# Attention scores begun before the last value block, four tiles of a quad handed to other engines, and a second norm issued later

## The chip, the cores and the metric

The kernel runs on one core of one Trainium2 chip. The metric is the device time of one execution in microseconds; the time of a kernel is the median over its runs. Engines are called PE (matmul; PEld is its weight load), DVE (VectorE), ACT (ScalarE), POOL (GpSimd) and SP (the queue that issues the DMAs).

## The reference

Two graph-attention layers are followed by one masked transformer layer over N = 4096 rows of D = 256, with 8 heads of 32. The change touches the transformer layer only.

```python
def _L1_gnn_ref(x, adj, w_qkv, w_proj, b_proj, w1, b1, w2, b2, g1, be1, g2, be2):
    n = x.shape[0]
    qkv = layer_norm(x, g1, be1) @ w_qkv
    qkv = qkv.reshape(n, 3, HEADS, HEAD_DIM)
    q, k, v = (qkv[:, 0], qkv[:, 1], qkv[:, 2])
    scores = jnp.einsum('nhd,mhd->hnm', q, k) * SCALE
    mask = (adj != 0)[None, :, :]
    scores = jnp.where(mask, scores, -jnp.inf)
    attn = jax.nn.softmax(scores, axis=-1)
    out = jnp.einsum('hnm,mhd->nhd', attn, v).reshape(n, DIM)
    x = x + out @ w_proj + b_proj
    h2 = layer_norm(x, g2, be2)
    ff = jax.nn.gelu(h2 @ w1 + b1) @ w2 + b2
    return x + ff
```

## The kernel before

The graph-attention layers take the first 1600 us and are left alone. `unshifted_transformer` then has three stages.

**q, k and v.** The rows are in eight blocks of 512 (`nb`). For each block the normed rows are turned (`ahead.turned`, PE transposes and an ACT copy into `hn`), and the PE forms k and then q (`i` = 1, 0; L1810), which ACT and DVE split into an fp16 head and remainder (`u_halves`, L1817 and L1818). SP writes these to `half_d` in DRAM and loads them back stacked for the scores (`u_k`, `u_q`, L1734); for the last three blocks all four copies come by DMA, for the others two come by DMA and DVE makes the other two (L1846). The values follow (L1829), and ACT copies them to `v_sb`. All eight PSUM banks serve this stage as one pool, `ps_q`. On SP the order is as written; the other engines' order is the scheduler's.

**Attention.** The order on every engine is written out by hand here. A quad is one query block of 512 rows with one head group of four heads (16 quads); a unit is one key tile of 128 in a quad (32 units a quad, 512 in all); each unit has two halves `u` of two heads. For each half the PE forms the scores (`u_ps`, eight matmuls, L1872; three buffers of two banks), ACT takes the exponential in place (L1882), and DVE multiplies by the mask into `u_e` (L1883; pool `work`, ten buffers). Two halves are treated otherwise in each quad: for tiles 0 and 16, first half, ACT writes the exponential to SBUF (L1885) and POOL multiplies it (L1886) by a mask that ACT made two units earlier (`keep_mask`, L1896).

The sums are split into parts of a quarter of the columns, which wait in the list `waiting` and are popped behind the scores, three in each half and sometimes four. `weigh` multiplies `u_e` by the values into `u_av`; `total` multiplies by ones into `u_dn`. For most pairs of tiles POOL first adds the two (`u_both`, L2095), and one total serves both; a pair for which `alone` holds gets two totals on the PE, straight from `u_e`:

```python
        def alone(mt):
            return mt // 2 % 8 == 7
```

At the end of a quad ACT copies `u_av` and `u_dn` out (L1920, L1937), and later DVE inverts the sums (L1946). `u_av` and `u_dn` have one bank each. In the last quad `load_early` brings the weights and rows for the next stage, and `rows_ready(k)` (two POOL products, L2016 and L2017) prepares the first two row blocks; the dictionary `ending` places this and the following steps.

**Output and feed-forward.** `project(k)` for the first two row blocks stands among the last sums of attention: 16 PE records (L2048), four DVE adds (L2056), then the second norm (DVE statistics L1514 and L1521, ACT square root L1526, DVE L1535 and L1543), and a POOL addition (L2065). `turn_first(c)` turns the two column halves of the first block through `u_av` (PE and ACT, L1556 and L1559). The feed-forward loop over eight blocks follows (L2186, L2193, L2206).

## Time and profile before

| | |
|---|---|
| time, median of 3 runs | 3123.89 us (3123.82 to 3124.47) |
| the profiled execution | 3124.94 us, span 3123.2 us |
| PE busy in the span | 3061.6 us (98%) |
| DVE busy | 2747.7 us (88%) |
| ACT busy | 2699.7 us (86%) |
| POOL busy | 1265.1 us (41%) |
| q/k/v stage | about 1602 to 1690 us |
| attention | 1693 to about 2863 us |
| feed-forward | from 2866 us |

Busy time is summed over stages with different limits, so it is read by stretch. In the groups of the profile a line gives the source line, engine, operation, what is written from what, count, busy time, mean length of one, and the idle time before it with what ended that. The timeline merges neighbours of one kind. The chain goes back from the last instruction to what released each step. A matmul with fp32 operands appears as two records.

### The profile page before, as it was taken

Reading aid. Unit: us, or ns where it says so; the run is one execution under the profiler, and the core shown is the slowest. Engines: PE = TensorE matmul, PEld = TensorE weight load, DVE = VectorE, ACT = ScalarE, POOL = GpSimd, SP = SyncE. Lnnn points to the kernel's source line nnn. Section 1 sums busy time; section 2 is a strip of 40 time slices with the busy share of each in tenths; the row PEclk is TensorE's granted clock in tenths of the full one; section 3 lists DMA queues with packets and bytes.
Section 4 is the critical chain, followed back from the end, with each engine's and each line's share of the span. In section 5 each row is a group of like instructions: output and inputs, shape, how many; then the busy total and the mean of one; then the engine's idle time right before and its main releaser. Section 6 shows DMA issues by size and latency. Waiting matters only on the chain.

```text
span 3123.2 us, 139201 instructions
## 1 busy us (share of the span) xinstructions
PE 3061.6 (98%) x63976; PEld 2713.3 (87%) x63976; DVE 2747.7 (88%) x3110; ACT 2699.7 (86%) x3370; POOL 1265.1 (41%) x568
## 2 busy tenths in 40 slices
PE   6999999999999999999999999999999999999998
PEld 5899999999889999999975888888888888887766
DVE  7999999999989999999985999999999999997220
ACT  6899999999899999999975999999999999996232
POOL 3300000000330000000002999999999999997110
PEclk8999999999999999999999999999999999999999
DMA  8666555431311213121145101010101110013210
GB/s 257 218 198 205 171 174 167 144 100 33 91 59 29 90 56 97 32 64 53 46 116 152 34 21 35 21 41 28 35 21 35 30 30 28 28 40 102 68 34 22
DMA packets 213171, 250.35 MB, mean 80 GB/s; under 512 B 89120, under 2 KB 133664, under 8 KB 212576
## 3 DMA queue, kind: packets, MB, share of 16 engines
q1 hardware_dynamic: 212576, 241.37, 25.1%
q8 instruction: 502, 8.22, 1.1%
q14 instruction: 93, 0.76, 0.1%
HBM read 198.84 MB, written 42.47 MB: 77 GB/s over the span
## 4 chain that ended last, share of the span: by engine, by line
PE 51%; ACT 1%; DVE 1%; issue 0%; DMA 0%; DVEq 0%; ACTq 0%
PE u_ps L1872 15%; PE u_av L1904 14%; PE u_dn L1904 8%; PE misc L2186 4%; PE misc L2206 4%; PE bank L1463 3%; PE misc L1810 2%; PE misc L1829 1%; ACT t L1122 1%; PE misc L2147 1%; PE misc L1556 0%; DVE t L1137 0%; DVE t L1124 0%; DVE u_e L1883 0%; PE u_ps L2048 0%
## 5 line engine op out<-in xcount | busy, mean ns | idle before, releaser
L1463 PE MATMUL bank<-vst,t 128*128 128x132 f16 x16384 | 1455.9, 220 | 3.6 <-DVE t L1137 2.7
L2095 POOL TENSOR_TENSOR u_both<-u_e 128x1024 f32<-128x1024 f32 x448 | 1047.9, 2388 | 805.1 <-DMA u_k<-half_d 775.6
L1463 PE MATMUL bank<-vst,mask 128*128 128x132 f16 (+1 forms) x10516 | 1372.3, 206 | 0.0
L1122 ACT ACTIVATE t<-s_b,g_terms 128x1024 int8<-128x1024 f32 x1234 | 1318.7, 1148 | 21.0 <-PE bank L1463 15.2
L1463 PEld LDWEIGHTS <-t 128*128 128x128 fp8e4 x16384 | 1186.3, 96 | 15.8 <-DVE t L1137 5.4
L1883 DVE SCALAR_TENSOR_TENSOR u_e<-u_mask,u_ps 128x1024 f32<-128x1024 uint8 x994 | 1131.5, 1213 | 26.8 <-ACT u_ps L1882 25.8
L1882 ACT ACTIVATE u_ps<-u_ps 128x1024 f32<-128x1024 f32 x994 | 996.4, 1008 | 93.0 <-PE u_ps L1872 33.6
L1463 PEld LDWEIGHTS <-mask 128*128 128x128 fp8e4 x10516 | 920.4, 98 | 0.0
L1137 DVE SCALAR_TENSOR_TENSOR t<-mask,t 128x2048 int32<-128x2048 int32 x256 | 587.9, 2296 | 74.8 <-ACT t L1122 66.4
L1872 PE MATMUL u_ps<-u_q,u_k 128*32 128x512 f16 x8192 | 632.4, 381 | 7.0 <-DVE u_e L1883 4.5
L1904 PE MATMUL u_av<-u_e,u_v 128*32 128x128 f32 x16384 | 602.9, 273 | 0.0
L1124 DVE TENSOR_SCALAR t<-s_b,g_terms 128x1024 fp8e4<-128x1024 f32 x814 | 590.1, 758 | 2.7 <-DMA s_b<-s_d 2.7
L1904 PEld LDWEIGHTS u_av<-u_e,u_v 128*32 128x32 f32 x16384 | 483.2, 110 | 120.6 <-issue 0.7
L1054 POOL TENSOR_TENSOR vst<-g_adj,vst 128x528 f16<-128x528 f32 x16 | 19.9, 1241 | 725.7 <-ACT g_big L1018 681.6
L1904 PE MATMUL u_dn<-u_both,u_ones 128*32 128x128 f32 x7168 | 279.2, 273 | 0.0
L1904 PEld LDWEIGHTS u_dn<-u_both,u_ones 128*32 128x32 f32 x7168 | 212.9, 110 | 52.1 <-issue 0.7
L1872 PEld LDWEIGHTS <-u_k 128*32 128x32 f16 x8192 | 229.5, 96 | 29.2 <-issue 8.9
L2193 ACT ACTIVATE u_hid<-misc,n_b 128x512 f32<-128x512 f32 x64 | 43.9, 687 | 140.3 <-PE misc L2186 140.3
L2206 PE MATMUL misc<-u_k,u_hid 128*128 128x256 f32 x512 | 111.8, 379 | 0.0
L2206 PEld LDWEIGHTS misc<-u_k,u_hid 128*128 128x128 f32 x512 | 96.7, 190 | 13.3 <-issue 0.5
L2186 PE MATMUL misc<-ln_cols,u_k 128*128 128x512 f32 x224 | 97.3, 592 | 0.0
L867 DVE TENSOR_SCALAR adj<-g_adj 128x1024 fp8e4<-128x1024 int32 x123 | 88.9, 723 | 3.8 <-DMA g_adj<-in_adj_dram 3.8
(186 smaller groups left out, 1919.2 us busy)
## 6 DMA issues: line engine op xcount, KB each, us to landing
g_adj<-in_adj_dram SPq DMA_DIRECT2D x123, 512.0 KB
s_b<-s_d SPq DMA_DIRECT2D x64, 512.0 KB
mask<-mask SPq DMA_DIRECT2D x128, 256.0 KB
u_mask<-mask SPq DMA_DIRECT2D x64, 256.0 KB
mask<-stage SPq DMA_DIRECT2D x48, 256.0 KB
half_d<-u_halves SPq DMA_DIRECT2D x32, 256.0 KB
u_q<-half_d SPq DMA_DIRECT2D x32, 256.0 KB
rows<-e_x SPq DMA_DIRECT2D x31, 256.0 KB
```

Of the source, the lines that this page charges most:

```text
L867: nc.vector.tensor_scalar(v.rearrange("p m r -> p r m"), loaded.pop((nb, c, i)), 1.0, -(2.0**-30), op0=ALU.min, op1=ALU.max, saturate=False,)
L1122: nc.scalar.activation(to.bitcast(I8), s, AF.Sign, bias=negd, scale=-1.0)
L1124: nc.vector.tensor_scalar(to, s, negd, -1.0, op0=ALU.is_ge, op1=ALU.mult, saturate=False)
L1137: nc.vector.scalar_tensor_tensor(both, m32.unsqueeze(1).to_broadcast(list(both.shape)), SIGNS, both, op0=ALU.bitwise_or, op1=ALU.bitwise_and,)
L1463: nc.tensor.matmul(to, left, right, start=k not in opened, stop=last)
L1872: nc.tensor.matmul(ps[r * O : (r + 1) * O, j, :], k_st[c][:, 2 * u + j, at : at + O], q_st[:, h, :], start=True, stop=True,)
L1882: nc.scalar.activation(ps, ps, AF.Exp, scale=SCALE)
L1883: nc.vector.scalar_tensor_tensor(e, mask, 0.0, ps, op0=ALU.not_equal, op1=ALU.mult)
L1904: nc.tensor.matmul(to[j * O : (j + 1) * O, at], lefts[j], es[j // 2][:, j % 2, at], start=first and part == 0, stop=last and part == PARTS ...
L2095: nc.gpsimd.tensor_tensor(both, es_of[i - 1][u], es_of[i][u], op=ALU.add)
L2186: nc.tensor.matmul(ph, w1_sb[:, k, f * P : (f + 1) * P], hn[:, k, :], start=(k == 0), stop=(k == DC - 1),)
L2206: nc.tensor.matmul(po[:, :D], hid[:, f, at : at + P], w2_sb[:, f, :], start=(f == 0), stop=(f == FC - 1),)
```

## The change

- **Scores earlier.** The values of the last row block are no longer formed in the q/k/v stage, but in the first units of attention (`last_values`: tiles 0 to 2 behind the scores of unit 1, tile 3 behind those of unit 2), through the banks of `u_av` and `u_dn`. Their inputs are kept in a `u_q` buffer (`hn_last`, and `wv_last`, loaded by two more DMAs). PSUM in the q/k/v stage becomes pools of six and two banks; the last block's k takes the six, its q the two. `work` moves to the right side of SBUF, where the buffers of the layers before were; `u_both` gets a pool of its own. `u_halves` has four buffers in place of three, and block 4's k joins those that come by DMA alone.
- **Other places in a quad.** The PE sums tiles 6, 7, 22 and 23 by itself in place of 14, 15, 30 and 31, and in the last quad tiles 30 and 31 too. POOL masks the second half of tiles 8 and 24 in place of the first half of tiles 0 and 16; the mask for it is made one unit ahead. `rows_ready(0)` moves from tile 15 of the last quad to tile 23.
- **Second norm later.** `project` is cut in two; the norm of the first block follows its projection as before, that of the second comes behind `turn_first(1)`.

```diff
-        if c == 0:
+        if to is not None:
+            self.hn[nb] = to
+        elif c == 0:
...
-            hv = qkv.enter_context(tc.tile_pool(name="u_hv", bufs=3))
-            ps_q = qkv.enter_context(tc.tile_pool(name="u_ps_q", bufs=8, space=PSUM))
+            hv = qkv.enter_context(tc.tile_pool(name="u_hv", bufs=4))
+            psums = [
+                qkv.enter_context(tc.tile_pool(name=f"u_ps_q{k}", bufs=n, space=PSUM))
+                for k, n in enumerate((6, 2))
+            ]
+            used = []
+            def bank(which=None):
+                used.append(None)
+                k = len(used) % 4 == 0 if which is None else which
+                return psums[k].tile([P, NB], F32, name="misc")
...
+            spare = blocks.tile([P, 4 * NB], F32, name="u_q")
+            hn_last = spare[:, : DC * NB].rearrange("p (c n) -> p c n", c=DC)
+            wv_last = spare[:, DC * NB : DC * NB + DC * D].rearrange("p (c e) -> p c e", c=DC)
...
+                if nb == 3:
+                    for c in range(DC):
+                        nc.sync.dma_start(
+                            wv_last[:, c], ahead.w_qkv[c * P : (c + 1) * P, 2 * D : 3 * D]
+                        )
...
-                        pq = ps_q.tile([P, NB], F32, name="misc")
+                        pq = bank(1 - i if nb + 1 == NNB else None)
...
-                for t in range(TB):
-                    pv = ps_q.tile([P, NB], F32, name="misc")
+                for t in range(TB) if nb + 1 < NNB else ():
+                    pv = bank()
...
-                            late = b >= NNB - 3
+                            late = b >= NNB - 4
...
-        work = scope.enter_context(tc.tile_pool(name="u_work", bufs=10))
+        work = scope.enter_context(tc.tile_pool(name="u_work", bufs=10, side="right"))
+        adds = scope.enter_context(tc.tile_pool(name="u_adds", bufs=6))
...
-            one = kept.pop((nb, c, mt), None) if u == 0 else None
+            one = kept.pop((nb, c, mt), None) if u == 1 else None
...
-        def alone(mt):
-            return mt // 2 % 8 == 7
+        def last_values(t):
+            at, name = (NNB - 1) * TB + t // 2 * 2, ("u_av", "u_dn")[t // 2]
+            if t % 2 == 0:
+                sums_of[name] = ps_a.tile([P, NB], F32, name=name)
+            to = sums_of[name]
+            for k in range(DC):
+                nc.tensor.matmul(
+                    to[:, t % 2 * D : (t % 2 + 1) * D],
+                    hn_last[:, k, t * P : (t + 1) * P],
+                    wv_last[:, k, :],
+                    start=(t % 2 == 0 and k == 0),
+                    stop=(t % 2 == 1 and k == DC - 1),
+                )
+            if t % 2 == 1:
+                nc.scalar.copy(
+                    v_sb[:, at : at + 2, :].rearrange("p t d -> p (t d)"), sums_of.pop(name)
+                )
+        def alone(i):
+            return units[i][2] // 2 % 8 == 3 or i + 2 >= len(units)
...
-            (units.index((NNB - 1, DC - 1, NT // 2 - 1)), 1): [lambda: rows_ready(0)],
+            (units.index((NNB - 1, DC - 1, 23)), 1): [lambda: rows_ready(0)],
...
                 lambda: project(0),
+                lambda: norm_rows(0),
             ],
             (last + 3, 0): [lambda: project(1)],
             (last + 3, 1): [lambda: turn_first(0)],
-            (last + 4, 1): [lambda: turn_first(1)],
+            (last + 4, 1): [lambda: turn_first(1), lambda: norm_rows(1)],
...
+        def norm_rows(k):
+            res = early[k][0]
             both = norms.moments(res)
...
-                    if u == 0 and i + 2 < len(units) and units[i + 2][2] % 16 == 0 and (
-                        units[i + 2] != (NNB - 1, DC - 1, NT // 2)
+                    for t in {2: (0, 1, 2), 4: (3,)}.get(2 * i + u, ()):
+                        last_values(t)
+                    if u == 0 and i + 1 < len(units) and units[i + 1][2] % 16 == 8 and (
+                        units[i + 1] != (NNB - 1, DC - 1, 24)
                     ):
-                        keep_mask(*units[i + 2])
-                    if i % 2 == 1 and not alone(mt):
+                        keep_mask(*units[i + 1])
+                    if i % 2 == 1 and not alone(i):
```

More of the change, by code (lines that the diff above doesn't have):

```diff
@@ L1596, in normed, with turned @@
         self.norms.normed(self.xs[nb], self.xs[nb], self.held.pop(nb))
-    def turned(self, nb, c, pt):
-        if c == 0:
+    def turned(self, nb, c, pt, to=None):
+        if to is not None:
+            self.hn[nb] = to
+        elif c == 0:
             self.hn[nb] = self.stage_p.tile([P, self.D // P, 512], F32, name="g_ft", tag="stage")
@@ L1798, in unshifted_transformer @@
                     for c in range(DC):
-                        ahead.turned(nb + 1, c, ps_q.tile([P, NB], F32, name="misc"))
+                        to = hn_last if nb + 2 == NNB else None
+                        ahead.turned(nb + 1, c, bank(), to)
+                if nb == 3:
[3 more added lines that the diff above has]
+                        )
                 if 2 < nb + 2 < NNB:
@@ L2088, in unshifted_transformer @@
                     es_of.setdefault(i, []).append(weights(*units[i], u))
-                    if u == 0 and i + 2 < len(units) and units[i + 2][2] % 16 == 0 and (
-                        units[i + 2] != (NNB - 1, DC - 1, NT // 2)
-                    ):
-                        keep_mask(*units[i + 2])
-                    if i % 2 == 1 and not alone(mt):
-                        both = work.tile([P, 2, NB], F32, name="u_both", bufs=6)
+                    for t in {2: (0, 1, 2), 4: (3,)}.get(2 * i + u, ()):
+                        last_values(t)
+                    if u == 0 and i + 1 < len(units) and units[i + 1][2] % 16 == 8 and (
+                        units[i + 1] != (NNB - 1, DC - 1, 24)
+                    ):
+                        keep_mask(*units[i + 1])
+                    if i % 2 == 1 and not alone(i):
+                        both = adds.tile([P, 2, NB], F32, name="u_both")
                         nc.gpsimd.tensor_tensor(both, es_of[i - 1][u], es_of[i][u], op=ALU.add)
@@ L2100, in unshifted_transformer @@
                     ready(total, i - 4, both_of.pop(i - 4))
-                if u == 1 and 0 <= i - 2 < len(units) and alone(units[i - 2][2]):
+                if u == 1 and 0 <= i - 2 < len(units) and alone(i - 2):
                     ready(total, i - 2, es_of[i - 2])
```

## The prediction

> **What bounds the kernel now.** I read the page's groups, the busy times by stretch, the timeline of VectorE (DVE), and the chain of work that ended last, in this order. A unit is one key tile of one quad (query block and head group); it has two halves, `u` = 0 and 1, of two heads each. The groups of the attention loop:

> ```profile
> L1883 DVE SCALAR_TENSOR_TENSOR u_e<-u_mask,u_ps 128x1024 f32<-128x1024 uint8 x994 | 1131.5, 1213 | 26.8 <-ACT u_ps L1882 25.8
> L1882 ACT ACTIVATE u_ps<-u_ps 128x1024 f32<-128x1024 f32 x994 | 996.4, 1008 | 93.0 <-PE u_ps L1872 33.6
> L2095 POOL TENSOR_TENSOR u_both<-u_e 128x1024 f32<-128x1024 f32 x448 | 1047.9, 2388 | 805.1 <-DMA u_k<-half_d 775.6
> ```

> The loop runs from 1693 to about 2850 us, so DVE's masking is busy 1131.5 of some 1157 us. The stretches show where the engines are not full:

> ```profile
> core 0: us, PE busy (x) PEld busy (x) DVE busy (x) ACT busy (x) POOL busy (x), PEclk, DMA share, GB/s
> 1602.00:1690.00 88.00, 88.00 (x310) 53.84 (x309) 53.23 (x126) 43.45 (x85) 0.00 (x0) 1.00 0.67 198
> 1690.00:1703.00 13.00, 6.75 (x111) 4.01 (x113) 7.05 (x7) 7.26 (x11) 2.77 (x2) 0.87 0.69 186
> 1711.80:1783.90 72.10, 72.10 (x2104) 59.08 (x2100) 70.58 (x63) 66.32 (x74) 70.24 (x31) 1.00 0.10 29
> ```

> The q/k/v stage (1602 to 1690) is full on the PE. The hand-over (1690 to 1703) is half empty on every engine. One quad, the last row, shows the PE at 72.10 of 72.10 and DVE at 70.58. DVE's timeline tells which of the two paces it (second column: length of the run, last: what ended the idle time):

> ```profile
> 1703.10 30.63 DVE L1883 SCALAR_TENSOR_TENSOR u_e<-u_mask,u_ps 128x1024 f32<-128x1024 uint8 x27 [0.72 <-ACT u_ps L1882]
> 1734.44 35.22 DVE L1883 SCALAR_TENSOR_TENSOR u_e<-u_mask,u_ps 128x1024 f32<-128x1024 uint8 x31 [0.71 <-ACT u_ps L1882]
> 1770.34 15.13 DVE L1883 SCALAR_TENSOR_TENSOR u_e<-u_mask,u_ps 128x1024 f32<-128x1024 uint8 x13 [0.69 <-ACT u_ps L1882]
> 1785.39 0.25 DVE L1946 RECIPROCAL u_inv<-u_dens 128x16 f32<-128x16 f32 x1
> ...
> 1806.65 35.19 DVE L1883 SCALAR_TENSOR_TENSOR u_e<-u_mask,u_ps 128x1024 f32<-128x1024 uint8 x31 [0.71 <-ACT u_ps L1882]
> 1842.56 15.02 DVE L1883 SCALAR_TENSOR_TENSOR u_e<-u_mask,u_ps 128x1024 f32<-128x1024 uint8 x13 [0.71 <-ACT u_ps L1882]
> ```

> Between the halves that GpSimd masks, DVE runs without a gap, one mask each (35.22 - 1.21) / 30 = 1.133 us. The PE needs less for a half: 0.43 us of scores and three parts of sums of 0.22, 1.09 us, with one extra part in each eight halves. So DVE paces these runs; a half given to GpSimd (a relief) saves 1.13 and loses 0.70 of idle, 0.43 net. Sixteen tiles take 1770.34 - 1734.44 = 35.90 us where no quad ends in between, and 1806.65 - 1770.34 = 36.31 where one does. The chain passes the same PE group at 1711.77 and, 15 quads later, at 2794.03: 72.15 us a quad. The hand-over in that chain (start, length, what):

> ```profile
> 1692.10 0.69 DVE u_halves L1818
> 1692.79 0.02 issue
> 1692.81 3.69 DMA half_d<-u_halves
> ...
> 1696.62 2.36 DVE u_e L1883 x2
> ...
> 1703.10 3.49 DVE u_e L1883 x3
> ```

> The first `u_e` waits for the last write of `half_d` to land: its memory was `u_halves`.

> [...] DVE paces quads in which the PE shows 72.10 of 72.10. [...] in the trace ScalarE (ACT) writes a relief half's exponentials to `u_e` first (L1885, 1.03 us), and then GpSimd multiplies (2.41 us). [...] L1883 has one input in each memory and takes 1,157 to 1,224 ns while POOL is 97% busy, so I move POOL's work without changing DVE's price. [...] after the 3.43 us wait at 1697.89, eight score matmuls took 1.05 us at 1699.02 in place of 0.62.

> **The change, part by part.**

> *1. Early first scores.* The PE reaches the last block's value matmuls (L1829) at 1686.94. Afterwards the first scores stand there. Their six PSUM banks were last used by block 7's k halves, two q-groups (3.4 us) earlier; and `u_e`, now on the right side, no longer lies on `u_halves`. Walking the queues from there, with durations of before:
> - ACT casts the last q piece (0.58) to 1687.75; DVE subtracts (0.69) to 1688.45. Score 1 is done at 1686.94 + 0.62; its exp (1.01) ends 1688.76; masks 1 to 3 start at 1688.8, 1689.9, 1691.1.
> - The PE does three score halves, then values of tiles 0 to 2 (0.87 each) from 1688.45, when q frees the bank: to 1691.1. Score 4 starts there; ACT first copies the values out (0.57), and exp 4 ends 1692.75: mask 4 starts at 1692.8 after 0.6 of idle, mask 5 at 1693.95.
> - Score 6 stands behind score 5 (0.43), the fourth values (0.87) and three parts (0.65): 1693.5. Behind ACT's second copy, exp 6 ends 1695.16; mask 6 starts at 1695.2.

> Before, mask 6 started at 1703.10 (the run after the 0.72 gap). From there both are paced by DVE: **7.9 us** gained. Bounds 7.4 and 8.4: one copy of 0.5 more in the way, or one less.

> What this needs lies beside other work. Two 128 KB loads of value weights and four more k loads (block 4) go to SP's queue in a stage with a DMA share of 0.67; they delay block 3's and block 6's `half_d` writes by 0.4 to 0.5 us of issue each, and block 4's k is read only after 16 tiles (36 us). Without that cover the PE would stop on a k load, 1 to 3 us. Four DVE copies of 0.7 fall away where DVE is 60% busy: nothing. The fourth `hv` buffer takes away a 1.5 us wait of ACT that the PE did not feel: nothing. The 6+2 split of banks keeps the reuse distance at eight tiles: nothing. POOL's first sum waits for the same `half_d` writes; they now leave after 1688.45 and land about 3.7 us later, at 1692.4, when the third mask ends.

> *2. Other places in the quad.* The same counts a quad: 62 masks on DVE, two on POOL, 28 sums on POOL, four tiles that the PE sums alone. Before, the relief (tile 0) falls on the end of a quad, right after ACT's two copies of `u_av` and `u_dn` come due (0.48 us of ACT each). ACT is then already what DVE waits for: the 13 masks at 1770.34 take 15.13 where 12 x 1.133 + 1.21 = 14.81, and 15.02 at 1842.56: 0.2 to 0.3 lost a quad. Moved to tile 8, the quad's end lies amid a DVE-paced run, where a score can start as soon as the mask three halves ahead is done: exp is ready 1.21 + 0.06 + 0.66 + 1.01 = 2.94 us after that mask starts, and is wanted after 3.40. A copy of 0.48, less the 0.21 that ACT is idle in each half, fits into 0.46. The reciprocal (0.17) stays. So a quad becomes 2 x 35.90 + 0.17 = 71.97, or about 71.85 if the second half also shortens the relief's idle: 0.18 to 0.30, I take 0.25, x 15 = 3.75. Tile 8 of the first quad is relieved too (31 reliefs, not 30): 0.43. Sum **4.2**, bounds 1 and 6.

> The wait that is added: `weigh` of tile 8 needs GpSimd's half one half later in the unit. Before, the product ended at 1735.93 and tile 16's values began at about 1739.25: 3.3 us of slack, so about 2.2 remain; POOL has just had the alone pair's 4.5 us free. Cost nothing. The Sign (0.53 of ACT) is moved, not added, but for one.

> *3. Last pair alone.* Two more totals less one: 32 PE records, 0.87 us, against a GpSimd sum that was late anyway; the PE has some slack in the last quad: **0.2 to 0.87** lost, I take 0.5. `rows_ready(0)` (two POOL products, 2.4 each) goes to tile 23, again into an alone pair's hole.

> *4. Later second norm.* At the end the ACT queue holds the second block's Sqrt ahead of the first block's turned copy:

> ```profile
> 2863.85 0.36 DVE L1521 BATCH_NORM_AGGREGATE n_mean<-n_stats 128x2 f32<-128x6 f32 x4
> 2864.24 0.30 ACT L1526 ACTIVATE n_mean<-n_mean,n_eps 128x4 f32<-128x4 f32 x1 [6.35 <-DVE n_mean L1521]
> 2864.45 0.76 ACT L1559 ACTIVATE u_q<-u_av,n_be,n_g 128x512 f32<-128x512 f32 x1
> ...
> 2866.95 0.28 PEld L2186 LDWEIGHTS misc<-u_q,u_k 128*128 128x128 f32 x1 [0.74 <-ACT u_q L1559]
> ```

> The transposes for the first copy ended at 2862.49, so without the Sqrt it runs 2862.5 to 2863.3. The PE's sums end at 2863.28, second transposes to 2863.7; ACT copies `u_den` (0.57) and turns the second half by about 2864.85. The second weight load of the feed-forward stage moves from 2866.95 to 2864.85: **2.1** gained (1.2 if the copy of `u_den` falls badly, 2.3 at most). Late next is the second block's norm, by some 0.8 us; its transposes come at 2884, so nothing. The first GELU waits behind it, with eight PSUM banks for the PE.

> Sum: 7.9 + 4.2 - 0.5 + 2.1 = 13.7. The profiled execution took 3124.94 us (span 3123.2), 1.05 above the median of the runs, 3123.89; I take the 13.7 from either: 3111.2 as profiled, **3110.2** as median.

> **Rivals.**
> - *Placement gives nothing:* DVE paces as before and the copies' cost turns up elsewhere. For it: the relief's 0.70 of idle stays in any place. Against: the boundary's extra 0.41 us is plainly in the trace. 3110.2 + 4.2 = 3114.4.
> - *The change doesn't do what it says at the start:* `u_e`, or a neighbour in its queue, still waits for the last `half_d` write (1692.4). Mask 1 then starts 3.6 later: 3113.8. For it: such a wait was there before. Against: the memory is another.
> - *Slower: a new PE wait at the end of each quad.* `u_av` has one buffer; the next quad's first values wait until ACT has copied it out. Before, eight parts of sums (alone pair, and the pair before) stood between; now four, some 1.7 us with the scores among them. The copy is ready about 2.2 us after the score ahead of it, so a stall of 0 to 0.3 is possible. If one more exp (0.92) stands before the copy, 1.2 a boundary, x 15 = 18 us: 3128.4. It decides from 0.93 us a boundary (13.7 / 15); against it, the copy at 1773.48 started at once behind its exp.

> **How the numbers follow.** Forecast 0.70, placement nothing 0.14, start not early 0.11, slower wait 0.05. The forecast's own bounds: best 8.4 + 6 - 0.2 + 2.3 = 16.5 (3107.4), worst 7.4 + 1 - 0.87 + 1.2 = 8.7 (3115.2). With the two rivals inside and a little beyond the best: 3106.5 to 3115.5. About 0.2% (6.2 us) is what a measurement of this kernel can tell from no change; the first three cases all gain more unless two go wrong together, so faster 0.93, same 0.04 (a part of the slower wait, or two rivals at once), slower 0.03.

> **What would show it.** First score near 1687, first mask near 1688.8, mask 6 near 1695.2, no DMA in the hand-over's chain; quads of 71.85 to 71.97 in the chain, with DVE's idle at tiles 8 and 24 alone; the first turned copy ahead of the second Sqrt and the feed-forward stage without a 2 us PE gap. A PE wait on `u_av` at quads' ends, on `u_e` at tile 8, or masks slower than 1.133 would prove it wrong.

## The result, and the profile after

The changed kernel takes **3110.35 us** (median of 6 runs, 3109.33 to 3111.24), the kernel before on the same chip 3124.18 us (3123.51 to 3126.1): ratio 0.9956, 95% interval 0.9944 to 0.9968. The forecast was 3110.2. The profiled execution took 3110.39 us with a span of 3108.6, 14.6 less than the span before. These are the groups of attention after the change (busy us, mean ns of one; then the idle before them and what ended it):

```profile
L1905 DVE SCALAR_TENSOR_TENSOR u_e<-u_mask,u_ps 128x1024 f32<-128x1024 uint8 x993 | 1127.9, 1210 | 23.8 <-ACT u_ps L1904 23.5
L1904 ACT ACTIVATE u_ps<-u_ps 128x1024 f32<-128x1024 f32 x993 | 995.7, 1009 | 83.9 <-PE u_ps L1894 29.5
L2142 POOL TENSOR_TENSOR u_both<-u_e 128x1024 f32<-128x1024 f32 x446 | 1044.4, 2387 | 768.8 <-DMA u_k<-half_d 768.7
L1894 PE MATMUL u_ps<-u_q,u_k 128*32 128x512 f16 x8192 | 634.4, 380 | 0.7 <-DVE u_e L1905 0.7
```

Every piece of work costs what it did: a mask 1210 ns (1213 before), an exponential 1009 (1008), a POOL sum 2387 (2388), a score matmul 380 (381). One mask has gone from DVE to POOL, and two sums have gone from POOL to the PE. The gain isn't in the price of the pieces, and must lie in where the work stands. The chain shows the start of attention (start, length, what):

```profile
1686.46 1.41 PE u_ps L1894 x24
1687.87 1.99 PE u_av L1952 x8
...
1694.02 1.02 ACT u_ps L1904
1695.06 3.50 DVE u_e L1905 x3
...
1703.74 0.87 PE u_av L1926 x32
...
2782.84 0.87 PE u_av L1926 x32
```

No DMA stands in the hand-over any more, and the group of 32 sums at 1703.74 is the one that stood at 1711.77 before (the sums of unit 7). Fifteen quads later the same group comes at 2782.84: (2782.84 - 1703.74) / 15 = 71.94 us a quad, before 72.15. DVE's timeline:

```profile
1692.35 2.35 DVE L1905 SCALAR_TENSOR_TENSOR u_e<-u_mask,u_ps 128x1024 f32<-128x1024 uint8 x2 [0.77 <-ACT u_ps L1904]
1695.06 13.80 DVE L1905 SCALAR_TENSOR_TENSOR u_e<-u_mask,u_ps 128x1024 f32<-128x1024 uint8 x12 [0.35 <-ACT u_ps L1904]
1709.46 35.34 DVE L1905 SCALAR_TENSOR_TENSOR u_e<-u_mask,u_ps 128x1024 f32<-128x1024 uint8 x31 [0.60 <-ACT u_ps L1904]
1745.49 31.78 DVE L1905 SCALAR_TENSOR_TENSOR u_e<-u_mask,u_ps 128x1024 f32<-128x1024 uint8 x28 [0.70 <-ACT u_ps L1904]
1777.20 0.24 DVE L1987 RECIPROCAL u_inv<-u_dens 128x16 f32<-128x16 f32 x1
1777.36 3.41 DVE L1905 SCALAR_TENSOR_TENSOR u_e<-u_mask,u_ps 128x1024 f32<-128x1024 uint8 x3
1781.47 35.16 DVE L1905 SCALAR_TENSOR_TENSOR u_e<-u_mask,u_ps 128x1024 f32<-128x1024 uint8 x31 [0.70 <-ACT u_ps L1904]
```

After the start, gaps stand only at tiles 8 and 24. The sixteen tiles with a quad's end in them take 1781.47 - 1745.49 = 35.98 us where they took 36.31. The gap ahead of 1709.46 is that of the one relief more, tile 8 of the first quad.

The earlier stages, which the change leaves alone, ended at another time in each execution (the first q/k/v matmul comes between 1601.2 and 1603.0 us in the 13 traces). So I count from that matmul (1602.58 before, 1601.93 after):

| us from the start of the q/k/v stage | before | after |
|---|---|---|
| start of mask 6 | 100.52 | 93.13 |
| start of the last exp | 1247.2 | 1236.3 |
| second feed-forward weight load | 1264.37 | 1251.69 |
| end of span | 1520.57 | 1506.67 |

So the 14.6 us of span are: the start 7.39, the loop from there to the last exp 3.5, the tail to the second weight load 1.8, the feed-forward stage 1.2, and 0.65 that had come before the change begins. The first of these varies with the kernel before: in the four traces that keep the old start (the kernel before, runs 1, 2 and 9) mask 6 lies at 99.10 to 101.02, while the changed kernel and all runs with its start as a whole have 93.13. The tail after the change:

```profile
2850.98 0.78 ACT L1559 ACTIVATE u_q<-u_av,n_be,n_g 128x512 f32<-128x512 f32 x1 [4.42 <-PE u_av L1556]
...
2852.10 0.66 PE L1556 MATMUL u_av<-ident,u_q 128*128 128x128 f32 x4
...
2853.47 0.29 ACT L1526 ACTIVATE n_mean<-n_mean,n_eps 128x4 f32<-128x4 f32 x1
2853.62 0.30 PEld L2233 LDWEIGHTS misc<-u_q,u_k 128*128 128x128 f32 x2 [0.84 <-ACT u_q L1559]
```

The turned copy (L1559) now precedes the square root (L1526), and the second transposes start without a wait. Before, they had waited 1.99 us, and that had a sequel. This is the wait in the kernel before, and then two stretches, the one that holds the wait and the one behind it (after the busy times comes the granted PE clock):

```profile
2865.26 0.82 PE L1556 MATMUL u_av<-ident,u_q 128*128 128x128 f32 x4 [1.99 <-ACT u_q L1559]
```
```profile
core 0: us, PE busy (x) PEld busy (x) DVE busy (x) ACT busy (x) POOL busy (x), PEclk, DMA share, GB/s
2862.21:2865.62 3.41, 1.42 (x30) 0.99 (x29) 3.01 (x14) 1.38 (x3) 0.00 (x0) 1.00 0.17 41
2865.62:2869.03 3.41, 3.41 (x7) 1.56 (x6) 0.56 (x2) 0.84 (x2) 2.71 (x2) 0.50 1.00 342
```

For 3.41 us the granted clock stood at 0.50; as an estimate, that takes at most (1 - 0.50) x 3.41 = 1.7 us of PE work. The same place after the change stands at 1.00. From the second weight load to the last matmul the feed-forward stage took 248.59 us before; in the changed kernel it takes 247.34, and the same in nine of the runs, in none of which the clock falls before that matmul. What follows the last matmul varies by up to 1.3 us between executions. To the end of the span the stage takes 254.98 in place of 256.20.

### The profile page after: what moved, and what is told of

Same layout as the page of the kernel before. It is cut to its first block, busy times and chain, and to the rows that moved or that the text cites. A ratio compares the mean times of both kernels' runs of the same rounds, so it can differ in the third digit from the quotient of the medians.

```text
span 3108.6 us, 139283 instructions
## 1 busy us (share of the span) xinstructions
PE 3056.0 (98%) x64008; PEld 2716.8 (87%) x64008; DVE 2744.2 (88%) x3105; ACT 2702.1 (87%) x3369; POOL 1263.6 (41%) x567
## 4 chain that ended last, share of the span: by engine, by line
PE 51%; ACT 1%; DVE 1%; issue 0%; DVEq 0%; ACTq 0%
PE u_ps L1894 15%; PE u_av L1926 14%; PE u_dn L1926 8%; PE misc L2253 4%; PE misc L2233 4%; PE bank L1463 3%; PE misc L1831 2%; ACT t L1122 1%; PE misc L1850 1%; PE misc L2194 1%; PE misc L1556 0%; DVE t L1137 0%; PE u_ps L2090 0%; DVE t L1124 0%; DVE u_e L1905 0%
## 5 line engine op out<-in xcount | busy, mean ns | idle before, releaser
L2142 POOL TENSOR_TENSOR u_both<-u_e 128x1024 f32<-128x1024 f32 x446 | 1044.4, 2387 | 768.8 <-DMA u_k<-half_d 768.7
L1905 DVE SCALAR_TENSOR_TENSOR u_e<-u_mask,u_ps 128x1024 f32<-128x1024 uint8 x993 | 1127.9, 1210 | 23.8 <-ACT u_ps L1904 23.5
L1904 ACT ACTIVATE u_ps<-u_ps 128x1024 f32<-128x1024 f32 x993 | 995.7, 1009 | 83.9 <-PE u_ps L1894 29.5
```

What stands on the lines that cost most here:

```text
L1904: nc.scalar.activation(ps, ps, AF.Exp, scale=SCALE)
L1905: nc.vector.scalar_tensor_tensor(e, mask, 0.0, ps, op0=ALU.not_equal, op1=ALU.mult)
L2142: nc.gpsimd.tensor_tensor(both, es_of[i - 1][u], es_of[i][u], op=ALU.add)
```

## The experiments

Theory: four separate gains that add up (scores no longer behind `half_d`; ACT's copies at a quad's end away from the relief; the second square root out of the way; the last pair nearly free). Rivals: the gains share a cause, or the new places help for another reason than the copies. First the three parts by themselves, each put into the kernel before.

**1. The norm alone**

```diff
                 lambda: project(0),
+                lambda: norm_rows(0),
...
-            (last + 4, 1): [lambda: turn_first(1)],
+            (last + 4, 1): [lambda: turn_first(1), lambda: norm_rows(1)],
```

> The kernel before with the later second norm alone. Theory A: the change took a 1.99 us PE wait ahead of the feed-forward stage away and, with it, a spell of slow PE clock just after that wait (0.50 granted from 2866 to 2868 us, 0.74 to 2870; about 1.3 us lost). It then gains 2.0 + 1.3 = 3.3 us: 3120.9. Rival: the slow clock has another cause (the stage's first DMAs, or chance), and the gain is the wait's alone: 2.0 us, 3122.2.

3120.97 us, ratio 0.9992 (0.9983 to 1.0). The interval reaches to no change; the profile tells more: the stretch from the last exp to the second weight load takes 15.09 us in place of 17.17, the transposes don't wait, the clock stays at 1.00, and the feed-forward stage takes 254.79 in place of 256.20. So 2.1 come with the norm and 1.4 with the clock.

**2. The places alone**

```diff
-            one = kept.pop((nb, c, mt), None) if u == 0 else None
+            one = kept.pop((nb, c, mt), None) if u == 1 else None
...
-            return mt // 2 % 8 == 7
+            return units[i][2] // 2 % 8 == 3 or i + 2 >= len(units)
...
-                    if u == 0 and i + 2 < len(units) and units[i + 2][2] % 16 == 0 and (
+                    if u == 0 and i + 1 < len(units) and units[i + 1][2] % 16 == 8 and (
```

> The kernel before with the other places in a quad alone (PE alone for tiles 6, 7, 22, 23 and the last pair; GpSimd masks the second half of tiles 8 and 24). Theory A: a quad takes 71.94 us as in the changed kernel, in place of 72.15, and the first quad has one relief more: 15 x 0.21 + 0.4 = 3.6 us, less up to 0.9 for the last pair: 3121 (2.7 to 3.6 gained). Rival: the shorter quads came from the other parts (another place of the buffers in memory, say), and the time stays at 3124.

3119.14 us, ratio 0.9987 (0.9981 to 0.9994). Sixteen tiles with a quad's end take 35.98 and 35.95 us, as in the changed kernel; from unit 7's sums to the last exp it takes 3.8 less. The last pair's extra total fell into the wait of the transposes, which shrank to 1.54 us, and the feed-forward stage took 254.93, without the slow clock.

**3. The early scores alone**: the changed kernel with `alone`, the relief and the norm as before.

> The changed kernel with the places in a quad and the norm put back: the early scores alone. Theory A: mask 6 starts 7.4 to 8.0 us earlier, and the time falls by as much, to 3116.5; quads of 72.15 us. Rival: the early scores are given back within the first quad (the late values and the copies crowd the start), and less than 6 us remain.

3117.18 us, ratio 0.998 (0.9972 to 0.9989). Mask 6 comes 93.13 us from the stage's start, to the hundredth as in the changed kernel, and 7.2 of the 7.39 are still there at the last exp (1240.0 against 1247.2). The stretches with a quad's end take 36.30 and 36.19 us, as before, so their shortening belongs to the places and not to the new buffers. The wait of the transposes is 1.98 again, the clock falls again, and the feed-forward stage takes 256.94. By medians the three parts give 2.8 + 4.6 + 6.6 = 14.0 us against 13.8 for the whole: they add up.

**4. `u_e` on the left again**, so that it may lie on `u_halves`:

```diff
-        work = scope.enter_context(tc.tile_pool(name="u_work", bufs=10, side="right"))
+        work = scope.enter_context(tc.tile_pool(name="u_work", bufs=10))
```

> The changed kernel with the pool of u_e on the left side again, where it lies on u_halves. Theory A: the first mask waits for the last write of half_d to land, at about 1691.9 in place of 1688.1; the next five then run without a gap, so mask 6 starts 2.5 us later (five masks of 1.13 behind 1691.9, against 1695.06) and the time rises by 2.5 us to 3112.9. Rival: freeing the PSUM banks was all that mattered, and the time stays at 3110.4.

3114.7 us, ratio 0.9973 (0.9964 to 0.9982), 4.4 above the changed kernel: dearer than expected. These are its DVE and PE timelines, and a stretch:

```profile
1691.73 5.76 DVE L1905 SCALAR_TENSOR_TENSOR u_e<-u_mask,u_ps 128x1024 f32<-128x1024 uint8 x5 [4.55 <-DMA u_k<-half_d]
1699.33 2.35 DVE L1905 SCALAR_TENSOR_TENSOR u_e<-u_mask,u_ps 128x1024 f32<-128x1024 uint8 x2 [1.84 <-ACT u_ps L1904]
```
```profile
1693.00 0.79 PE L1894 MATMUL u_ps<-u_q,u_k 128*32 128x512 f16 x8 [2.92 <-DVE u_e L1905]
...
1695.11 1.91 PE L1952 MATMUL u_dn<-u_q 128*128 128x256 f32 x4
```
```profile
core 0: us, PE busy (x) PEld busy (x) DVE busy (x) ACT busy (x) POOL busy (x), PEclk, DMA share, GB/s
1694.00:1696.00 2.00, 1.86 (x10) 0.94 (x10) 2.00 (x3) 1.61 (x2) 0.65 (x1) 0.50 0.95 214
```

The first mask waits for the DMA, as claimed, so the side of the pool is needed. But the PE then stood for 2.92 us, its clock fell to 0.50, the last values took 1.91 us in place of 1.06, and DVE waited 1.84 more: mask 6 is 4.9 us later, not 2.5. The expectation had counted the wait and not the clock.

**5. One PSUM pool in the q/k/v stage**, in place of six and two banks:

```diff
-                for k, n in enumerate((6, 2))
+                for k, n in enumerate((8,))
...
-                k = len(used) % 4 == 0 if which is None else which
-                return psums[k].tile([P, NB], F32, name="misc")
+                return psums[0].tile([P, NB], F32, name="misc")
```

> The changed kernel, but the q/k/v stage takes its eight PSUM banks from one pool again (every tile in turn) in place of six and two. The prediction's step 1 says that the first scores start as soon as the PE is through the last value matmuls of block 7's forerunner because their six banks were last used two groups earlier. Theory A (the split matters): with one pool the banks of the first scores include those that the last q pieces used, so the first score waits for DVE's subtraction of the last q head; first score about 1.2 us later relative to the start of the stage, mask 6 (the run after the first gaps) 0.8 to 1.5 us later than in the changed kernel (93.1 us after the stage's start becomes 94 to 94.6), the rest unchanged: about 3111.4 us. Rival B (the u_e memory alone is what lets the scores start early): mask 6 within 0.3 us of the changed kernel, same time.

3112.59 us, ratio 0.9962 (0.995 to 0.9975), 2.2 above the changed kernel. Its PE timeline:

```profile
1687.31 1.48 PE L1893 MATMUL u_ps<-u_q,u_k 128*32 128x512 f16 x24 [1.40 <-DVE u_halves L1838]
```

The first scores wait 1.40 us for DVE's last subtraction, and mask 6 lies at 94.53, just as much later. (The other 0.8 of the medians' difference was not followed up.) The early start needs both: the memory of `u_e` and six banks last used two groups earlier.

**6. PE's own pairs moved back, GpSimd's masked half not**: in `alone`, `% 8 == 3` becomes `% 8 == 7`, and `rows_ready(0)` returns to tile 15.

> The changed kernel, but the pairs that the PE sums alone are tiles 14, 15, 30, 31 again (and the last pair), while GpSimd still masks the second half of tiles 8 and 24. POOL is busy 70.4 of 72 us a quad, and a pair that the PE sums alone leaves it one hole of 4.5 us. Theory A (hole and masked half belong together): the masked half now stands in POOL's queue behind sums that come late, GpSimd's product is late, the PE's values of tile 8 wait for it, and the stop comes in each half of a quad: 74 to 77 us a quad in place of 71.94, 3140 to 3190 us in all, with PE idle time put down to POOL u_e. Rival B (only the place of the masked half away from a quad's end matters, POOL has enough slack anywhere): 71.9 to 72.1 a quad, 3110 to 3112 us.

3221.09 us, ratio 1.0312 (1.0295 to 1.033). GpSimd's masked halves in the changed kernel, and then in this one:

```profile
L1908 POOL TENSOR_TENSOR u_e<-u_e,u_one 128x1024 f32<-128x1024 f32 x31 | 73.9, 2384 | 26.3 <-ACT u_e L1907 25.5 <-ACT u_k L1747 0.8
```
```profile
L1908 POOL TENSOR_TENSOR u_e<-u_e,u_one 128x1024 f32<-128x1024 f32 x31 | 73.0, 2355 | 0.0
L1926 PE MATMUL u_av<-u_e,u_v 128*32 128x128 f32 x16384 | 695.2, 279 | 68.6 <-POOL u_e L1908 68.6
```

In the changed kernel POOL stands ready and waits 26.3 / 31 = 0.85 us for each exponential. Here POOL comes straight from its sums (no idle), late, and the PE waits 68.6 us in all, 2.2 each. A stretch of 10 us around one of these waits:

```profile
core 0: us, PE busy (x) PEld busy (x) DVE busy (x) ACT busy (x) POOL busy (x), PEclk, DMA share, GB/s
1793.00:1795.00 2.00, 0.00 (x0) 0.00 (x0) 2.00 (x2) 0.81 (x2) 2.00 (x2) 1.00 0.31 113
1795.00:1797.00 2.00, 1.99 (x44) 1.74 (x48) 0.13 (x1) 0.25 (x1) 2.00 (x1) 0.68 0.41 129
1797.00:1799.00 2.00, 2.00 (x36) 1.66 (x32) 1.14 (x1) 0.76 (x1) 2.00 (x2) 0.50 0.03 8
```

After the wait the clock falls to 0.50, and DVE does 1.3 us of work in the next 4. That happens behind 19 of the 31 waits, for 3.41 us each: as an estimate, these take up to 19 x 1.7 = 32 us of PE work. The waits alone are 68.6 of the 110.7 us lost; by this estimate the slow clock can account for most of the rest. (The mean clock of the whole span is 0.986, in the changed kernel 0.996.) The prediction's "POOL has just had the alone pair's 4.5 us free. Cost nothing" holds on that condition alone: hole and masked half move together or not at all. The expectation had the mechanism, and too small a number: like that of run 4 it left the clock out.

**7. GpSimd masks the first half of tiles 8 and 24**: `u == 1` becomes `u == 0` where the kept mask is taken.

> The changed kernel, but GpSimd masks the first half of tiles 8 and 24 in place of the second half. Theory A (a quad's end away from the masked half is the gain; which half is a detail): 71.9 to 72.05 a quad in place of 71.94, total 3110 to 3112 us. Rival B (the second half is what brings the gain, because it shortens DVE's gap of 0.70 us or gives GpSimd's product its time): the idle of DVE at tiles 8 and 24 grows by 0.1 to 0.3 us each or the PE waits on POOL u_e, 72.15 to 72.5 a quad, 3113.5 to 3118 us.

3111.71 us, ratio 0.9963 (0.9949 to 0.9977). Sixteen tiles take 35.99 or 35.93 us with a quad's end and 35.95 without; the last exp comes 1236.2 us after the stage's start (1236.3 in the changed kernel). Which half is taken doesn't matter for the time.

**8. The last pair added by GpSimd**: `or i + 2 >= len(units)` leaves `alone`.

> The changed kernel, but the last pair of tiles (30, 31 of the last quad) is added by GpSimd again and gets one total, as in the kernel before. Tests step 3 of the prediction, a loss of 0.2 to 0.87 us. Theory A (the extra total costs time): last exp to second feed-forward weight load 15.38 us in the changed kernel becomes 14.5 to 15.2, total 0.2 to 0.9 less, about 3110. Rival B (the extra total stands where the PE would wait for GpSimd's sum of the last pair anyway): the total waits for POOL u_both, and the stretch grows by 0.3 to 2 us, about 3111 to 3112.

3113.46 us, ratio 0.9964 (0.995 to 0.9978): 3.1 slower than the changed kernel. (The expectation's "as in the kernel before" is wrong: there the PE summed tiles 30 and 31 by itself.) POOL and PE near the end, first of the changed kernel, then of this one:

```profile
2841.29 2.39 POOL L2057 TENSOR_TENSOR u_q<-u_q,u_mask 128x1024 f32<-128x1024 f32 x1
...
2845.84 3.72 PE L2090 MATMUL u_ps<-u_k,u_q 128*128 128x256 f32 x16
```
```profile
2836.42 9.38 POOL L2142 TENSOR_TENSOR u_both<-u_e 128x1024 f32<-128x1024 f32 x4
...
2845.74 2.36 POOL L2057 TENSOR_TENSOR u_q<-u_q,u_mask 128x1024 f32<-128x1024 f32 x1
...
2848.15 5.41 PE L2090 MATMUL u_ps<-u_k,u_q 128*128 128x256 f32 x16 [2.46 <-POOL u_q L2057]
```

Two more sums (the last pair's two halves) stand before the products for the second row block; the second projection waits 2.46 us for the product and then takes 1.7 us longer, at a clock of 0.50 from 2850 to 2852. Last exp to second weight load is 18.4 us in place of 15.38. Rival B named POOL's sum, but not the place of the wait: what came late is not the total, but the products that are queued behind the sum on POOL.

**9 and 10. ACT's two copies at a quad's end cut to 32 of their 512 columns** (these two kernels leave the other columns of the sums out), in the kernel before and in the changed one:

```diff
-                num = tail.tile([P, NB], F32, name="u_num", bufs=2)
-                nc.scalar.copy(num, sums_of["av"])
+                num = short[0]
+                nc.scalar.copy(num[:, :32], sums_of["av"][:, :32])
...
-            den = tail.tile([P, NB], F32, name="u_den")
-            nc.scalar.copy(den, sums_of["dn"])
+            den = short[1]
+            nc.scalar.copy(den[:, :32], sums_of["dn"][:, :32])
```

> The kernel before with ACT's two copies at the end of a quad (u_av and u_dn) cut to 32 of their 512 columns; the other columns of the attention sums are left out and stand at one. Tests the cause given in step 2: before, sixteen tiles take 35.91 us inside a quad and 36.31 or 36.19 where a quad ends, because those copies (0.48 us each) come where ACT is what DVE waits for. Theory A (the copies' length is the cause): the stretches with a quad's end in them fall to 35.9 to 36.0 us, 0.2 to 0.35 a quad, 3 to 5 us in all, 3119 to 3121 us. Rival B (it is the order: the PE's own four tiles or the masked half at a quad's end): they stay at 36.2 to 36.3, the total within 1 us of the kernel before.

> The changed kernel with ACT's two copies at the end of a quad cut to 32 of their 512 columns; the other columns of the attention sums are left out and stand at one. Theory A (after the change the copies fit into ACT's slack): stretches with a quad's end stay within 0.1 of 35.97 us, total 0 to 1.2 us less than the changed kernel. Rival B (the copies still cost as much as before and the gain of the new places is of another kind): stretches with a quad's end fall by 0.2 to 0.35 us, 3 to 5 us in all.

3119.85 us, ratio 0.9986 (0.998 to 0.9993), and 3110.41 us, ratio 0.9952 (0.9935 to 0.9969). With short copies in the kernel before, the stretches with a quad's end fall from 36.31 and 36.19 to 36.01; in the changed kernel they go from 35.98 and 35.96 to 35.95. So the length of the copies is most of what the kernel before paid at each quad's end, and the change hides it almost wholly. (Of the 4.1 us that run 9 gains by medians, its trace has 3.1 in the loop; the rest is at the start, where its mask 6 lies at 99.10 in place of 100.52.) DVE's timeline with short copies in the kernel before:

```profile
1769.77 14.83 DVE L1886 SCALAR_TENSOR_TENSOR u_e<-u_mask,u_ps 128x1024 f32<-128x1024 uint8 x13 [0.69 <-ACT u_ps L1885]
...
1805.78 29.54 DVE L1886 SCALAR_TENSOR_TENSOR u_e<-u_mask,u_ps 128x1024 f32<-128x1024 uint8 x26 [0.71 <-ACT u_ps L1885]
```

The 13 masks after the relief take 14.83, where they took 15.13, and 12 x 1.133 + 1.21 = 14.81 is the pace of DVE. The same run also shows that a slow clock does not follow from a wait's length alone:

```profile
2861.08 0.66 PE L1556 MATMUL u_av<-ident,u_q 128*128 128x128 f32 x4 [1.98 <-ACT u_q L1559]
```
```profile
core 0: us, PE busy (x) PEld busy (x) DVE busy (x) ACT busy (x) POOL busy (x), PEclk, DMA share, GB/s
2856.14:2859.55 3.41, 2.96 (x56) 1.97 (x54) 2.52 (x8) 0.00 (x0) 1.34 (x1) 1.00 0.02 6
2859.55:2862.96 3.41, 1.87 (x7) 0.98 (x8) 2.04 (x10) 1.81 (x4) 0.82 (x1) 1.00 0.69 213
2862.96:2866.38 3.42, 3.42 (x9) 1.52 (x8) 0.00 (x0) 2.55 (x3) 3.42 (x2) 1.00 0.57 176
```

It is the same wait of 1.98 us, and the clock stays at 1.00. The last section shows why the three stretches begin and end where they do.

**11. The PE's own pairs and GpSimd's masked half moved on by four tiles**: the PE sums tiles 10, 11, 26, 27, and GpSimd masks the second half of tiles 12 and 28 (`% 8 == 5`, `% 16 == 12`).

> The changed kernel with hole and masked half moved on together by four tiles: the PE sums tiles 10, 11, 26, 27 alone (and the last pair), GpSimd masks the second half of tiles 12 and 28, and the two products for the last stage go to tile 27 of the last quad. Theory A (any place away from a quad's end serves): 71.9 to 72.0 a quad as in the changed kernel's 71.94, 3110 to 3112 us. Rival B (the gain is that of a place half way between two quad ends, with as much run on one side as on the other; nearer to the next end, four tiles after the masked half, POOL's sums or ACT's copies collide again): 72.1 to 72.3 a quad, 3113 to 3116 us.

3112.79 us, ratio 0.9965 (0.9951 to 0.9979). Stretches with a quad's end take 36.16 and 36.04 us, those without 35.9; the last exp comes 1.6 later than in the changed kernel. That is rival B's direction, at less than its price. With the end of the quad at the relief the excess over 35.91 is 0.40 and 0.28, four tiles after the relief 0.25 and 0.13, eight tiles after it 0.07 and 0.05. In these three places the copies are hidden the better the longer DVE has run since the last gap. What is worked off in those tiles (ACT's lag or the PE's list of waiting parts) was not taken apart.

## Why the prediction was right, by its steps

| step | predicted | measured | by what |
|---|---|---|---|
| 1 early scores | 7.9 | 7.39 | mask 6, in the change and by itself |
| 2 other places | 4.2 | 3.51 | unit 7 to the last exp |
| 3 last pair | -0.5 | -0.29 | tail 15.09 with the norm alone, 15.38 with all |
| 4 later norm | 2.1 | 2.08 | tail 17.17 before, 15.09 with the norm alone |
| PE clock in the feed-forward | none | 1.22 | 256.20 to 254.98 |
| before the change begins | none | 0.65 | start of the q/k/v stage |
| sum, of span | 13.7 | 14.6 | |

By medians the gain is 13.83. The mechanism of each step held. But the four priced terms come to 12.7, not 13.7: two were too large by 1.2 together, the price for the last pair was 0.2 too high, and a gain of 1.2 that was not foreseen made up for the difference. That the median lies within 0.2 us of the forecast is in part luck.

- **Step 1** was 0.5 too large. Mask 1 came where the walk had put it (1688.10 + 0.65 of earlier start = 1688.75, predicted 1688.8); the walk gave each of four value tiles 0.87 us, and they took 0.92, 0.92 (the mean of two), 0.96 and 1.06, 0.37 more in all; the fourth and fifth scores took 0.97 together in place of 0.86. Score 6, and with it mask 6, stands behind all of these: 0.48 of the 0.5 are durations taken from a steadier part of the kernel. How much there was to gain also depends on the execution: measured from mask 6 in the other traces with the old start it would be 6.0 to 7.9.
- **Step 2**: the cause that it gave is shown by runs 9 and 10. The size: by the chain a quad takes 72.15 before and 71.94 after, 0.21 less in place of 0.25; 15 x 0.21 + 0.43 = 3.6. The idea that the second half shortens the gap at the relief fell: the gaps were 0.69 to 0.71 before and are 0.69 to 0.74 now (one of 0.94), and run 7 has the same pace with the first half and gaps of 0.62 to 0.71. In the changed kernel four of 29 stretches are 0.1 to 0.25 longer than their like, in the kernel before none; the reason is open.
- **Step 2's unpriced wait** (POOL's product for tile 8) cost nothing, and run 6 shows what carried that: the hole just ahead of it.
- **Step 3** compared the extra total only with itself. Its 0.3 lies within the bounds, but run 8 shows the alternative at 3.1: without it, moving the pairs would have made the products for the next stage late.
- **Step 4** came out at its size; up to 0.2 of the 2.08 belong to the clock, since the same tail with the same wait takes 16.99 in run 9, without a slow stretch. "Late next is the second block's norm" is so (square root at 2853.47), and the PE doesn't wait for it. What the step left out is the clock. The prediction had the slow clock in view behind the wait of 3.43 us at the start, but not behind the 1.99 us that this step removes; of the three traces that have a wait of 1.98 or 1.99 us there, two show a slow stretch behind it.
- **The rivals**: the first mask does not wait for `half_d`; the placement does give; no PE wait on `u_av` appears (idle of the PE before its `u_av` sums 0.0 us in all, before `u_ps` 0.7 in place of 7.0). The slower case did not come at its place, but one like it was near: run 6, two lines away, loses 111 us. Two small sums of the slower case are off: 3110.2 + 18 is 3128.2, not 3128.4, and 13.7 / 15 is 0.91 us a boundary, not 0.93; nothing hangs on them.

## What to carry to other kernels

Where several engines are nearly full (here the PE, DVE at 98% and POOL at 97% of a quad), price a move by what else comes due at that place on every queue, and keep together what depends on each other: the hole in GpSimd's queue and the work that uses it. Small recurrent work of one engine (here two copies at each quad's end) was nearly free where the pacing engine had run for eight tiles without a gap, and cost 0.3 to 0.4 us where a gap had just been. Here a wait of the PE cost more than its length (1.99 us, and another 1.2 to 1.4 at the clock of 0.50 behind it), and an estimate that adds or removes one should keep a term for the clock after it.

## What the runs showed of the hardware

This tells the two equal waits apart. In the kernel before, the 1.99 us lie in one window (2862.21 to 2865.62). In run 9 the window's edge at 2859.55, 340 steps behind its slow stretch at 1699.02, divides the 1.98 us into 0.45 and 1.54, and the clock stays at 1.00. As an estimate from these numbers, a wait of 1.99 us at a time that chance sets falls into one window in (3.41 - 1.99) / 3.41, or 4 cases of 10; here it then cost 1.2 to 1.4 us.
